# A perceiver layer pair on one core: top-query selection by index search, and experts chosen from un-normalised logits

## The chip, the cores and the metric

The kernel runs on one core of one Trainium2 chip. The metric is the device time of one launch in microseconds (us); 702.21 is the median of three runs (706.4, 702.21, 701.24).

A core has TensorE (PE: matmuls; PEld: its weight loads), VectorE (DVE), ScalarE (ACT), GpSimd (POOL) and SyncE (SP), each with a queue of its own that it works off in order, and 16 DMA engines. Matmul results go to eight PSUM banks of 128 x 512 float32.

## The reference, cut to what matters

Two batches of 256 rows, width 256, float32 throughout. Six residual sub-layers: cross-attention, a state-space layer, a spectral layer, a second cross-attention, a sparse self-attention, a mixture of experts. The change lies in the last two.

```python
# sparse self-attention, on xn = layernorm(x)
Q, K, V = proj(wq, bq), proj(wk, bk), proj(wv, bv)       # 16 heads of 16
scores = einsum('bhqd,bhkd->bhqk', Q, K) * scale
u = int(log(L))                                          # 5
top_u = top_k(scores.max(axis=-1), u)[1]
q_sel = take_along_axis(Q, top_u[..., None], axis=2)
attn = softmax(einsum('bhud,bhkd->bhuk', q_sel, K) * scale)
ctx = einsum('bhuk,bhkd->bhud', attn, V)
padded = zeros((B, H, L, d_k)).at[bi, hi, top_u].set(ctx)
x = x + (padded.transpose(0, 2, 1, 3).reshape(B, L, D) @ wo.T + bo)
...
# mixture of experts, on xn = layernorm(x)
logits = einsum('btd,ed->bte', xn, Wr)                   # 8 experts
probs = softmax(logits)
topk_vals, topk_idx = top_k(probs, 2)
router_weights = topk_vals / topk_vals.sum(-1, keepdims=True)
h = silu(einsum('btd,efd->btef', xn, W1))                # DFF 1024
y = einsum('btef,edf->bted', h, W2)
x = x + einsum('bte,bted->btd', gate, y)
```

## The kernel before

**Stages.** Layer 0's cross-attention over 4,096 keys fills the first 405 us, with batch 0's state-space layer woven in. Then come the other sub-layers up to the router, written as Python generators, one step up to each `yield`: stream `a` for batch 1 (state space, spectral, `context_layer`, `self_attention`, `router`), stream `b` for batch 0 (spectral onwards) and stream `m` (a matrix for the spectral layer). The string `ORDER` (L42) says whose step is issued next; a letter `w` issues a filler (`at_work`, L1543: a matmul whose result nobody reads). Instructions issued so keep this order on their engines (`in_order`). What comes behind, in the block of the experts, is placed by the framework's scheduler and may move ahead of it.

**Self-attention** (`self_attention`, L985). The rows are normalised (`normalised`), turned so that channels lie on partitions (`turned`: four transposes to PSUM and a copy), and projected (`ps_aqk`; query and key for half of the heads each time, weights packed in the tile `more`). Two masked copies of the queries make eight heads' scores from 32-partition matmuls (`ps_am`, 16 instructions of 256 columns); VectorE reduces each bank to its maxima (`reduce_max` into `m`, 16 a batch). `m` is turned (`ps_mt`) to 16 heads x 256 rows (`mt`). MAX8 finds the five highest, MATCH_REPLACE8 marks them, a scan numbers the marks, a matmul (`ps_st`) spreads them over 16 x 5 places, a compare gives `picked` (places x rows). `picked` is turned to `S`; a matmul gathers the rows of `xn` (`ps_xs`), another projects them (`ps_qs`). The scores stand with queries on partitions (`ps_sc`), so the maximum (`least`), exp and total run along the row, and the result is turned again (`ps_et`) before the values (`ps_ob`), the output weights (`ps_ow`) and the matmul that puts rows back (`ps_wo`). VectorE adds that to `x`.

**Router and dispatch** (`router`, L1527; L1579 on). The new rows are normalised into `xn5`, turned, projected to eight logits. With both batches done, the best two experts are found in two rounds over four row tiles (L1597 to L1604; `rank` breaks ties), matmuls with a triangle of ones count each row's place (`ps_n`), and for the first three experts (`DIRECT`) a compare and a matmul gather the rows of all four tiles (`direct`, `ps_xs`). Rows for the others go by eight indirect DMAs from POOL's queue to `x_slots` in DRAM and are fetched block by block.

**Experts.** Ten blocks of 128 rows: one for each of eight experts, and two of shared overflow parts. `hidden(k)` (L1749), then `output(k)` (L1789). Fourteen of the 32 weight halves (1 MB each, issued on SP's queue) are loaded ahead, into seven homes as these come free: `ctx0, ctx1, Q, K0, K2, K1, V1`, for experts 0 to 6 (L1505). `K1` held batch 0's attention weights in `context_layer`, `K2` is `more`. The other 18 halves go where a used one lay.

The planner's order for the streams is a fixed string; no due times are computed while the program is built.

Of the kernel before, what the change touches and what calls it, by code (L numbers as in the profile page):

```python
# [13 lines left out]
P = 128  # L14
# [4 lines left out]
NG = 4  # L19
# [24 lines left out]
        "mmabwbmmmabbaaaambamaamabmmmmmamabaamwmmmaaaaaaaabmmabababbbabaabwbbaaabwwaabbba",  # L44
        "abaabbbababaawaaaabbaaaaabbbaaaaaabaaaaaaaaaabbaaaaaaaaababaaaaaaabaaaaaaaaaaaaa",
        "aabaaaaaaabaaabaaaaaaaaaabbbaaaaaabaaaaabbababaabaaabaaaaaaabaaabbbbbabbbbabaaaa",
        "bbaaaababbbbaaaababababbaaababbabbbaaaabaaabababaaaaaaaabababababbaaabbaaabbbaba",
        "abbbbaabbbbaaaaaabaaabbbbbbaaaaaabbbaaaaaaaababaabbbaaaaababbbbaaaaaaaaawwwawaba",
        "waawwbaawbwbaaaaabaaaaaaawaabaaaaabaaaaaababaaabbaaabwwababaawabaabbbaabbaaabbaa",
        "bbabaabwbbwbbaaaawbbbaawwaaaaaaba",  # L50
# [16 lines left out]
def layers(ctx: ExitStack, tc: tile.TileContext, d: dict, out: bass.AP, general: bool):  # L67
# [244 lines left out]
    rank = route.tile([P, E], F32, tag="rank", name="rank")  # L312
# [6 lines left out]
    def route_constants(zeros):  # L319
        nc.gpsimd.memset(above, 1.0)  # L320
        nc.gpsimd.affine_select(
            out=above, in_=above, pattern=[[1, P]], compare_op=ALU.is_gt, fill=0.0, base=0, channel_multiplier=-1
        )
        nc.gpsimd.memset(ones, 1.0)
        for t, step, base in ((first_slot, P, 0), (rank, -1, E), (further, 1, 0), (beyond, ROOM, P)):
            nc.gpsimd.iota(
                t, pattern=[[step, t.shape[1]]], base=base, channel_multiplier=0, allow_small_or_imprecise_dtypes=True
            )
        nc.gpsimd.memset(zeros, 0.0)
        for k in range(NB):  # L330
            nc.gpsimd.dma_start(out=x_slots[k * P : (k + 1) * P, :], in_=zeros)
# [355 lines left out]
    nat = {}  # L687
# [130 lines left out]
    def context_layer(b, bank):  # L818
# [27 lines left out]
        room = STATE["more"][:, 1536:] if b else large("K1", "weights")  # L846
        pT = [room[:, 512 * i : 512 * (i + 1)].rearrange("p (c q) -> p c q", c=2) for i in range(4)]
# [74 lines left out]
    def picking(pool):  # L922


        expand = pool.tile([H, P], F32, tag="expand", name="expand")
# [30 lines left out]
        theirs = pool.tile([P, 2, P], F32, tag="theirs", name="theirs")  # L956
# [10 lines left out]
        which = pool.tile([1, P], F32, tag="which", name="which")  # L967
        biases = STATE["more"][:1, 1024 : 1024 + 2 * D]
        w = which.rearrange("p (g n) -> p g n", g=NG)
        nc.gpsimd.memset(which, -1.0)  # L970
# [6 lines left out]
        for u in range(TOP_Q):  # L977
            nc.gpsimd.memset(w[:, :, u : 4 * TOP_Q : TOP_Q], float(u + 1))
        turned_rows = pool.tile([P, 5], F32, tag="nth", name="nth")
        PICK.update(  # L980
            expand=expand, own=own, theirs=theirs, parity=parity, rowed=[which] + [biases[:, i * P : (i + 1) * P] for i in range(4)], turned=turned_rows,
            nth=turned_rows[:, :1], qb=turned_rows[:, 1:3], kb=turned_rows[:, 3:5],
        )

    def self_attention(b, bank):  # L985
# [17 lines left out]
        v, m = part(2, D), part(2, H)  # L1003
        mt, left, number = part(NQ + 8), part(NQ + 8), part(NQ)
        picked, S, XT = part(NQ), part(2, P), part(2, P)
        ve.tensor_tensor(of(b), of(b), rows[:, A1_BO, :].unsqueeze(1).to_broadcast([P, 2, D]), ALU.add)
        yield
        if b == 0:
            ps = bank("ps_nth")
            for i in range(5):  # L1010
                te.matmul(
                    ps[:, i : i + 1], lhsT=PICK["rowed"][i], rhs=ones[:1, :1], start=True, stop=True
                )
            yield
            ve.tensor_copy(PICK["turned"], ps[:, :5])
            yield
        for g in range(2):
# [24 lines left out]
            if g == 0:  # L1042
# [8 lines left out]
                yield  # L1051

        ve.memset(mt[:H, NQ:], LOWEST)
        ps = bank("ps_mt")
        for qt in range(2):
# [5 lines left out]
        ve.max(top, mt[:H])  # L1061
        ve.memset(top[:, TOP_Q:], LOWEST)
        ve.match_replace(left[:H], top, mt[:H], -LOWEST)
        ve.tensor_tensor(left[:H], left[:H], mt[:H], ALU.not_equal)
        yield
        ve.tensor_tensor_scan(
            number[:H], ones[:H, :1].to_broadcast([H, NQ]), left[:H, :NQ], 0.0, ALU.mult, ALU.add
        )
        ve.tensor_mul(number[:H], number[:H], left[:H, :NQ])
        yield  # L1070
        ps = bank("ps_st")
        te.matmul(ps[:, :NQ], lhsT=PICK["expand"], rhs=number[:H], start=True, stop=True)
        yield
        ve.tensor_scalar(picked, ps[:, :NQ], PICK["nth"], None, ALU.is_equal)
        yield
        ps = bank("ps_s")
        for t in range(2):
            te.transpose(ps[:, t * P : (t + 1) * P], picked[:, t * P : (t + 1) * P], ident)
        yield
        ve.tensor_copy(S.rearrange("p t n -> p (t n)"), ps[:, : 2 * P])  # L1080
        yield
        ps = bank("ps_xs")
        for c in range(2):
            for t in range(2):
                te.matmul(
                    ps[:, c * P : (c + 1) * P], lhsT=xn[:, t, c * P : (c + 1) * P], rhs=S[:, t, :],
                    start=(t == 0), stop=(t == 1),
                )
        yield
        ve.tensor_copy(XT.rearrange("p c n -> p (c n)"), ps[:, : 2 * P])  # L1090
        yield
        ps = bank("ps_qs")
        for g in range(2):
            for c in range(2):
                te.matmul(
                    ps[:, 64 * g : 64 * g + 64], lhsT=PICK["wq"][:, c, g * P : (g + 1) * P], rhs=XT[:, c, 64 * g : 64 * g + 64],
                    start=(c == 0), stop=(c == 1),
                )
        yield
        QS = S[:, 0, :]  # L1100
        ve.tensor_tensor(
            QS.rearrange("p (g n) -> p g n", g=2), ps[:, :P].rearrange("p (g n) -> p g n", g=2),
            PICK["qb"].unsqueeze(2).to_broadcast([P, 2, 64]), ALU.add,
        )
        QS = QS.rearrange("p (g s n) -> p g s n", g=2, s=2)
        ve.tensor_tensor(QS, QS, PICK["own"].unsqueeze(1).to_broadcast([P, 2, 2, 32]), ALU.mult)
        yield
        ps = bank("ps_sc")
        for g in range(NG):
            te.matmul(  # L1110
                ps[32 * g : 32 * g + 32, :NQ], lhsT=QS[:, g // 2, g % 2, :], rhs=KT[g // 2], start=True, stop=True
            )
        yield
        least = small.tile([P, 1], F32, tag="m1", name="least")
        ve.reduce_max(least, ps[:, :NQ], axis=AX.X)
        ve.tensor_scalar_mul(least, least, -1.0)
        yield
        e = XT.rearrange("p c n -> p (c n)")
        total = small.tile([P, 1], F32, tag="nb", name="total")
        se.activation(e, ps[:, :NQ], AF.Exp, bias=least, accum_out=total)  # L1120
        yield
        ve.reciprocal(total, total)
        ps = bank("ps_et")
        for t in range(2):
            te.transpose(ps[:, t * P : (t + 1) * P], e[:, t * P : (t + 1) * P], ident)
        yield
        ve.tensor_copy(S.rearrange("p t n -> p (t n)"), ps[:, : 2 * P])
        yield
        ps = bank("ps_ob")
        for c in range(2):  # L1130
            for t in range(2):
                te.matmul(
                    ps[:, c * P : (c + 1) * P], lhsT=v[:, t, c * P : (c + 1) * P], rhs=S[:, t, :],
                    start=(t == 0), stop=(t == 1),
                )
        yield
        ve.tensor_tensor(XT, ps[:, : 2 * P].rearrange("p (c n) -> p c n", c=2), PICK["theirs"], ALU.mult)
        yield
        ps = bank("ps_ow")
        for c in range(2):  # L1140
            te.matmul(ps[:, :D], lhsT=XT[:, c, :], rhs=a1_wo[:, c, :], start=(c == 0), stop=(c == 1))
        yield
        OW = QT[0][0]
        se.mul(OW, ps[:, :D], total)
        yield
        ps = bank("ps_wo")
        for t in range(2):
            te.matmul(ps[:, t * D : (t + 1) * D], lhsT=picked[:, t * P : (t + 1) * P], rhs=OW, start=True, stop=True)
        yield
        ve.tensor_tensor(of(b), of(b), ps.rearrange("p (t e) -> p t e", t=2), ALU.add)  # L1150
        yield
# [375 lines left out]
    def router(b, bank):  # L1527
        yield from normalised(of(b), xn5[:, 2 * b : 2 * b + 2, :])
        xnT = XNT(b)
        yield from turned(xn5[:, 2 * b : 2 * b + 2, :], xnT, bank("ps_tr"))  # L1530
        ps = bank("ps_r")
        for t in range(2):
            project_rows(ps[:, t * E : (t + 1) * E], xnT, t, wr)
        yield
        ve.tensor_copy(logits[:, 2 * b : 2 * b + 2, :], ps[:, : 2 * E].rearrange("p (t e) -> p t e", e=E))
        yield

# [5 lines left out]
    def at_work(n):  # L1543

        ps = bank("ps_work")
        for _ in range(n):
# [6 lines left out]
            spectral_layer(1, bank), later((context_rows, 1)), context(1, bank), self_attention(1, bank), router(1, bank),  # L1553
        ),
        "b": chain(
            spectral_layer(0, bank), later((context_rows, 0)), context(0, bank), self_attention(0, bank), router(0, bank),
# [22 lines left out]
    with pool("ffn", 1) as one:  # L1579
        gathered = large("P", "gathered")  # L1580
        room = big.tile([P, 4368], F32, tag="V0", name="room")

        warm = small.tile([P, 1], F32, tag="warm", name="warm")
# [442 lines left out]
```

## Time and profile before

| | us |
|---|---|
| median of three runs | 702.21 |
| the profiled execution | 701.64 |
| its span, first to last instruction | 699.9 |
| layer 0, up to | 405 |
| batch 1's second cross-attention ends, about | 540 |
| last of the score reductions ends | 564.4 |
| first expert matmul | 604.0 |
| first of eight row scatters | 602.0 |
| last block's output begins | 682.1 |

The page's slices are a fortieth of the span each. In a table of stages, PE busy time comes from matmuls whose ends are modelled, and `(x...)` counts instructions; a float32 matmul stands as two records. `PEclk` is the share of its clock that TensorE was granted. The chain of waits is followed back from the last instruction; "issue" in it is time in which an engine waited for nothing that the profile shows. Lines of most instructions here are those of one helper (L190), so groups are told apart by their tiles.

### The profile page before, as it was taken

To read this page: it belongs to the slowest core of one execution; us is meant where nothing else is said; L and a number is where in the kernel's file an instruction comes from. 1 tells how busy PE (TensorE), PEld (TensorE's weight loads), DVE (VectorE), ACT (ScalarE), POOL (GpSimd) and SP (SyncE) were. 2 spreads that over 40 slices of the span, in tenths; PEclk is the share of its full clock that TensorE was granted. 3 is DMA by queue.
4 is the path that set the end of the run, shared out by engine and by line. 5 is a ranking of instruction groups with operands and counts; after the bars stand their busy time and mean duration, and the time that the engine had idled before them with its cause. 6 is when DMAs were issued, how large, how long until landed. Compare 5 with 4: busy or idle time off the path is not lost.

```text
span 699.9 us, 15840 instructions
## 1 busy us (share of the span) xinstructions
PE 665.7 (95%) x6528; PEld 448.2 (64%) x6528; DVE 289.2 (41%) x716; ACT 365.6 (52%) x478; POOL 102.9 (15%) x170
## 2 busy tenths in 40 slices
PE   8999999999999999999999999999999888899994
PEld 6555555665455665555555577877877666899852
DVE  2221332121122465445445248765666865601112
ACT  3667655756767657767876847746333013111220
POOL 8400022300000000000002000124434000410012
PEclk9999999999999999999999999999999969999999
DMA  6520353310220001110010344000732406189982
GB/s 211 152 51 3 78 154 91 95 54 9 49 47 22 2 2 31 41 38 17 2 46 3 122 122 120 1 1 1 253 108 88 154 0 241 54 303 331 310 274 81
DMA packets 40178, 65.83 MB, mean 94 GB/s; under 512 B 6657, under 2 KB 26545, under 8 KB 39969
## 3 DMA queue, kind: packets, MB, share of 16 engines
q1 hardware_dynamic: 34608, 52.06, 23.8%
q0 software_dynamic: 3488, 10.83, 5.0%
q10 hardware_dynamic: 2000, 1.84, 0.8%
q8 instruction: 54, 0.88, 0.5%
q14 instruction: 28, 0.22, 0.1%
HBM read 52.12 MB, written 4.46 MB: 81 GB/s over the span
## 4 chain that ended last, share of the span: by engine, by line
PE 88%; DVE 6%; ACT 3%; issue 2%; DMA 1%; SPq 0%; DVEq 0%; ACTq 0%
PE av L190 21%; PE ps L190 21%; PE ps_y L1794 5%; PE ps_v L190 5%; PE ps_k L190 5%; PE ps_s L190 5%; PE ps_h L1754 4%; PE ps_in L190 2%; PE ps_ht L190 2%; DVE states L190 2%; DVE arest L190 1%; PE ps_work L190 1%; PE ps_q L190 1%; PE yps L190 1%; PE ps_h L1766 1%
## 5 line engine op out<-in xcount | busy, mean ns | idle before, releaser
L190 ACT ACTIVATE exps<-ps 128x1024 f32<-128x1024 f32 x256 | 248.0, 1021 | 121.1 <-PE ps L190 118.6
L190 PE MATMUL ps<-qk,KB 32*128 32x256 f32 x2048 | 156.8, 401 | 2.5 <-DVE mp L190 1.6
L190 PE MATMUL av<-exps,V 128*32 128x256 f32 x2048 | 137.6, 385 | 0.3 <-ACT exps L190 0.3
L190 PEld LDWEIGHTS ps<-qk,KB 32*128 32x128 f32 x2048 | 99.8, 184 | 51.9 <-issue 41.0
L190 PEld LDWEIGHTS av<-exps,V 128*32 128x32 f32 x2048 | 53.5, 109 | 66.5 <-issue 39.9
L190 DVE TENSOR_TENSOR_SCAN states<-decay,ps_in 128x256 f32<-128x256 f32 x64 | 40.2, 671 | 21.0 <-PE ps_in L190 21.0
L190 DVE COPY V<-ps_v 128x512 f32<-128x512 f32 x28 | 19.4, 692 | 63.5 <-PE ps_v L190 61.6
L190 DVE COPY qk<-ps_k 128x512 f32<-128x512 f32 x28 | 19.3, 689 | 63.3 <-PE ps_k L190 42.3
L1794 PE MATMUL ps_y<-w,room 128*128 128x256 f32 (+1 forms) x256 | 39.2, 380 | 2.8 <-issue 2.5
L190 PEld LDWEIGHTS ps_v<-l_wv,ctxT 128*128 128x128 f32 x256 | 30.9, 191 | 10.4 <-issue 8.1
L190 PE MATMUL ps_v<-l_wv,ctxT 128*128 128x128 f32 x256 | 36.4, 287 | 0.4 <-ACT head L190 0.4
L1794 PEld LDWEIGHTS ps_y<-w,room 128*128 128x128 f32 (+1 forms) x256 | 28.6, 151 | 11.2 <-issue 6.2
L190 PE MATMUL ps_k<-ctxT,wkc 128*128 128x512 f32 x64 | 35.3, 638 | 0.0
L1754 PE MATMUL ps_h<-room,w 128*128 128x128 f32 x256 | 32.1, 283 | 2.7 <-issue 2.6
L1774 ACT ACTIVATE room<-ps_h 128x512 f32<-128x512 f32 x16 | 9.4, 597 | 47.3 <-PE ps_h L1754 30.5
L190 PE MATMUL ps_s<-xn,ctxT 128*128 128x256 f32 x128 | 33.4, 383 | 0.0
L190 POOL TENSOR_TENSOR weights<-weights 128x512 f32<-128x512 f32 x15 | 19.0, 1268 | 97.0 <-ACT weights L190 96.8
L1754 PEld LDWEIGHTS ps_h<-room,w 128*128 128x128 f32 x256 | 30.9, 198 | 3.6 <-issue 3.4
L190 ACT ACT_TABLE_LOAD x16 | 20.5, 1283 | 15.6 <-DVE least L190 14.8
L190 PEld LDWEIGHTS ps_s<-xn,ctxT 128*128 128x128 f32 x128 | 23.5, 190 | 5.8 <-issue 3.0
L190 POOL TENSOR_TENSOR more<-more 128x512 f32<-128x512 f32 x15 | 19.0, 1267 | 24.2 <-ACT more L190 24.1
L190 ACT ACTIVATE more<-more 128x512 f32<-128x512 f32 x16 | 10.1, 630 | 23.4 <-DVE more L190 23.4
(387 smaller groups left out, 814.1 us busy)
## 6 DMA issues: line engine op xcount, KB each, us to landing
w<-in_moe_w SPq DMA_DIRECT2D x32, 1024.0 KB
KB<-qk SPq DMA_DIRECT2D x224, 32.0 KB
ctxT<-in_ctxT POOLq DMA_DIRECT2D x4, 512.0 KB
ctxT<-in_ctxT SPq DMA_DIRECT2D x1, 2048.0 KB
x_slots<-O POOLq DMA_DIRECT2D x14, 128.0 KB
ctxT<-in_ctxT SPq DMA_DIRECT2D x3, 512.0 KB
y_slots<-room ACTq DMA_DIRECT2D x8, 128.0 KB
rows<-in_rows POOLq DMA_DIRECT2D x1, 896.0 KB
```

Of the source, the lines that this page charges most:

```text
L190: i = getattr(self.engine, name)(*args, **kw)
L1754: nc.tensor.matmul(ps[fc // 4][:, (fc % 4) * P : (fc % 4 + 1) * P], lhsT=weights[k, 0, 0][0][:, c, fc * P : (fc + 1) * P], rhs=xT[k][:, c, :],
L1766: nc.tensor.matmul(ps[i][r, :], lhsT=xT[k][:, c, r], rhs=weights[k, j, 0][0][:, c, 512 * i : 512 * (i + 1)], start=(c == 0), stop=(c == 1),)
L1774: nc.scalar.activation(to[i], ps[i], AF.Silu)
L1794: nc.tensor.matmul(ps[r, :D], lhsT=hT[k][:, fc, r], rhs=weights[k, j, 1][0][:, fc, :], start=(fc == 0), stop=(fc == NF - 1),)
```

## The change

The queries are no longer found again from gathered rows. After the maxima, an index search gives each head's five row numbers; these are spread over the 80 places by a product and a matmul with ones, and compared with the rows' own numbers (`place`): that is `S` at once. Queries are projected for all rows beforehand (`q`) and selected by `S`. The scores are made with keys on partitions, so that exp's output goes into the value matmul without a turn; the (negated) maximum, known from the search, is added by a matmul, and the totals come from a matmul with ones. The residual is added in PSUM (`new`), by a matmul with the identity.

The logits come ahead of the norm: `wr` less its column means makes the mean drop out, and the row's scale doesn't change which experts are highest. They are the sum of the old rows' logits (`old`, the turned rows before attention) and the picked places' own (`owr`, the output weights times the router's). The scale (`inverse`) enters in the softmax. Each batch chooses, counts and gathers inside its own stream; batch 0's gather for the three direct experts lies in `K1`'s old room until batch 1's is added. `ORDER` is a new string: 306 letters `a` for 311, 157 `b` for 158, 20 `m` as before, 5 `w` for 24; the two runs of four fillers around `ps_n` are gone, too. Nothing in layer 0 or in the experts' blocks is edited.

```diff
@@ picking
-        expand = pool.tile([H, P], F32, tag="expand", name="expand")
+        masks = acts.tile([P, 2, D], F32, tag="O0", name="masks").rearrange("p c n -> p (c n)")
+        expand = masks[:H, :P]
...
+    def self_weights(bank):
+        ps = bank("ps_nth")
+        for i in range(4):
+            te.matmul(ps[:, i : i + 1], lhsT=PICK["rowed"][i], rhs=ones[:1, :1], start=True, stop=True)
+        for c in range(2):
+            te.matmul(ps[:, E : 2 * E], lhsT=ones, rhs=wr[:, c, :], start=(c == 0), stop=(c == 1))
...
+        yield from turned(a1_wo, woT, bank("ps_woT"))
+        ps = bank("ps_owr")
...
@@ self_attention, after the value projection of the first half
+                ps = bank("ps_aq")
+                for t in range(2):
+                    project_rows(ps[:, t * D : (t + 1) * D], xnT, t, PICK["wq"])
+                yield
+                se.copy(q, ps.rearrange("p (t e) -> p t e", t=2))
+                yield
+                yield from turned(of(b), old, bank("ps_old"))
@@ self_attention, after mt
-        ve.max(top, mt[:H])
-        ve.memset(top[:, TOP_Q:], LOWEST)
-        ve.match_replace(left[:H], top, mt[:H], -LOWEST)
...
+        ve.max(top, mt[:H, :NQ])
+        ve.max_index(at, top, mt[:H, :NQ])
+        ve.tensor_scalar_mul(top, top, -1.0)
...
+        te.matmul(ps[:, :P], lhsT=ones[:H, :], rhs=spread[0], start=True, stop=True)
+        yield
+        for t in range(2):
+            ve.tensor_scalar(S[:, t, :], ps[:, :P], PICK["place"][:, t : t + 1], None, ALU.is_equal)
...
+        for t in range(2):
+            for g in range(2):
+                te.matmul(
+                    sc[:, t * P + 64 * g : t * P + 64 * g + 64], lhsT=KT[g][:, t * P : (t + 1) * P],
+                    rhs=QS[:, 64 * g : 64 * g + 64], start=False, stop=(t == 1 and g == 1),
+                )
+        pk = bank("ps_pk")
+        for t in range(2):
+            te.transpose(pk[:, t * P : (t + 1) * P], S[:, t, :], ident)
+        yield
+        e = QT[1][1]
+        se.activation(e, sc[:, : 2 * P], AF.Exp)
+        ve.tensor_copy(picked, pk[:, : 2 * P])
...
-        se.activation(e, ps[:, :NQ], AF.Exp, bias=least, accum_out=total)
...
+        ps, new = bank("ps_lg0"), bank("ps_new")
+        for t in range(2):
+            project_rows(ps[:, t * E : (t + 1) * E], old, t, PICK["wr"])
...
+        te.matmul(new.rearrange("p (t e) -> p t e", t=2), lhsT=ident, rhs=of(b), start=True, stop=False)
...
+        pr, po = bank("ps_or"), bank("ps_ow")
...
+        se.activation(root, total, AF.Sqrt)
...
-    def router(b, bank):
...
+    def attention_and_router(b, bank):
+        lg, new = yield from self_attention(b, bank)
...
+        for t in range(2):
+            ve.max(two[:, t, :], logits[:, 2 * b + t, :])
+        ve.tensor_copy(best[:, ts, :TOP_E], two[:, :, :TOP_E])
+        for t in range(2 * b, 2 * b + 2):
+            ve.match_replace(rest[:, t, :], best[:, t, :], logits[:, t, :], -LOWEST)
+        ve.tensor_tensor(chosen[:, b, :2, :], rest[:, ts, :], logits[:, ts, :], ALU.not_equal)
+        yield
+        nr = bank("ps_n")
...
+        for t in range(2):
+            ve.tensor_scalar(
+                xn5[:, 2 * b + t, :], new[:, t * D : (t + 1) * D], mv[:, t, 0:1], r[:, t : t + 1], ALU.subtract, ALU.mult
+            )
+        se.copy(of(b), new.rearrange("p (t e) -> p t e", t=2))
...
+        for k in range(1, DIRECT):
+            spots(b, k)
+            yield
+            ps = gather(b, k, bank)
+            yield
+            gathered_to(b, k, ps)
...
+    def gathered_to(b, k, ps):
+        first = XS["room"][:, k * D : (k + 1) * D]
+        if b:
+            ve.tensor_tensor(place_of_x(k), first, ps[:, :D], ALU.add)
+        else:
+            se.copy(first, ps[:, :D])
@@ the experts' block
-        for i in range(TOP_E):
-            of_these = rest if i else lg
-            nc.vector.reduce_max(best[:, i, :], of_these, axis=AX.X)
...
-        at_work(4)
-        ps = bank("ps_n")
...
-        direct(0)
...
+        num = XS["counts"]
```

## The prediction

> **What bounds the kernel now.** First the page: engines, the clock row and the chain.
>
> ```profile
> PE 665.7 (95%) x6528; PEld 448.2 (64%) x6528; DVE 289.2 (41%) x716; ACT 365.6 (52%) x478; POOL 102.9 (15%) x170
> ...
> PEclk9999999999999999999999999999999969999999
> ...
> PE 88%; DVE 6%; ACT 3%; issue 2%; DMA 1%; SPq 0%; DVEq 0%; ACTq 0%
> ```
>
> TensorE carries the whole program, and one slice of forty has a lower clock. The diff leaves everything up to 405 us alone (layer 0) and everything after the first hidden matmul. So next, busy time by stage for what lies between (columns: window, its length, then PE, PEld, DVE, ACT, POOL, clock, DMA share, GB/s):
>
> ```profile
> sum 135.00, PE 130.44 PEld 106.03 DVE 87.50 ACT 68.41 POOL 38.03; mean PE 21.74 PEld 17.67 DVE 14.58 ACT 11.40 POOL 6.34
> 560.00:564.00 4.00, 1.51 (x10) 1.08 (x10) 4.00 (x8) 0.00 (x0) 0.00 (x0) 1.00 0.00 0
> 564.00:568.00 4.00, 3.50 (x14) 2.83 (x14) 3.54 (x12) 0.00 (x0) 0.00 (x0) 0.62 0.00 0
> 568.00:578.00 10.00, 9.62 (x41) 7.12 (x40) 3.43 (x12) 1.85 (x3) 0.00 (x0) 0.50 0.05 3
> 615.00:640.00 25.00, 25.00 (x167) 23.50 (x167) 2.55 (x6) 4.18 (x7) 2.50 (x5) 0.98 0.98 339
> 640.00:680.00 40.00, 40.00 (x326) 30.96 (x324) 4.51 (x10) 8.02 (x14) 1.91 (x3) 1.00 0.93 310
> ```
>
> The sum is of 405 to 540: TensorE is dense there. From 540 it is not: VectorE is full in 560 to 564, and then TensorE runs at half clock for some 14 us. Last, the chain of waits from 540 (start, length, what):
>
> ```profile
> 539.75 0.98 PE ps_total L190 x8
> ...
> 541.70 3.04 PE ps_work L190 x14
> ...
> 559.16 5.20 DVE arest L190 x9
> ...
> 595.38 1.28 PE ps_n L190 x10
> ...
> 598.49 5.36 PE ps_xs L190 x48
> ...
> 603.96 4.91 PE ps_h L1754 x43
> 608.87 0.37 issue
> ```
>
> Three marks follow from it: C = 539.75, where batch 1's cross-attention is summed; R = 564.36, where the last score reduction ends (559.16 + 5.20); T = 603.96, the first hidden matmul. The prediction is where C, R and T fall.
>
> **C: from 405 to the end of cross-attention.** I laid both order strings against the generators' yields, letter by letter. When batch 1's last `weigh` is called, batch 0 has been given 15 of its 16 score reductions before, and 8 after. TensorE loses, ahead of C: `ps_nth` 1.20, the second `ps_aqk` 1.74, two `ps_am` at 1.08, `ps_av` 1.92, and three filler letters (14 records took 3.04, so 0.43 for two): 8.3 us. It gains `self_weights`: 12 records of one to eight columns at 0.12 (`ps_nth`'s own 1.20 for ten), the turned output weights 0.72 (`ps_tr`), eight records for their product 0.97 (`ps_r`): 3.1. As TensorE is 97% dense, C moves by 5.2, to 534.5. The other bounds: the new order may fill worse or better than the 4.6 us idle in 135; I take plus or minus 3. POOL's mask building loses five small fills and gains one fill and one iota; its 2.6 busy us in 425 to 450 wait for nothing: nothing, and under 1 us if uncovered.
>
> **R: from C to the last reduction.** Before, C to the first masked query (549.17) took 9.5. After it is the same steps; batch 0's query, key and old-row projections (1.73 + 0.57 + 1.74) fit in TensorE's wait for the norm, which fillers held; I add 0.5. So masked queries start at 544.5. From there VectorE has in order: 22 reductions at 0.62 (17 were 10.5 us busy), 13.6; four masked queries, 2.0; batch 1's value sum 0.68; batch 0's `mt` copy 0.41, search 1.47 (below), two places 0.56, masked selected queries 0.45: 19.2. Before, the like stretch (549.2 to 564.4) held 14.5 of VectorE work in 15.2; with two hand-overs to TensorE more I add 2 and get R = 565.8. So R stays: what C wins goes into reductions that came out from under cross-attention.
>
> The search is MAX8 (0.42 in its row), an index find that the trace doesn't show, a negation 0.15 and two products of 16 rows, 0.22 each. MATCH_REPLACE8 on the same row took 0.40 with a value load of 0.08; the find is bounded by 0.2 (a tiny instruction) and 1.2 (three passes of 0.40); I take 0.45, for it too is one pass.
>
> **T: from R to the first hidden matmul.** Before this is 39.6. Batch 1's chain after, each by its nearest row: turn 0.38, copy 0.41, search 1.47, places' matmul 0.3, compare 0.56, queries by selection 0.97, mask 0.45, scores 0.9, exp 0.47, values 1.05, mask 0.41, output and router rows 1.3, scaling 0.47, logits 0.44, choice of experts 1.3 (seven instructions at 0.17 to 0.20), norm statistics 1.6 beside the rank matmuls 0.8, number and root 0.2, compare 0.56, normalise 0.74, gather 0.97, copy 0.42: 15.4. Two more compares, gathers and copies overlap to 4.5. About 30 hand-overs at 0.05 are 1.5; one table load, for exp after the other batch's root, 1.28 (bounds 0 and three, 3.8). Batch 0's tail, which the order sets ahead of it, takes 1.7 at the start and 1.8 in between. Sum 26.2: T = 592.0.
>
> What went: second transposes, the gather of rows before projecting, the row maximum, the logits' detour over the normalised rows (transpose, copy, projection: about 2.2), the two-round choice (592.6 to 595.3), one third of the dispatch, and the half clock, worth some 6. ScalarE gains three copies at 0.58 and a root at 0.20 a batch; it is busy 13 of 76 us behind 540, so nothing, and 2 if each stood in a chain. TensorE's extra work, 6 us a batch (query projection 1.73, old rows turned 0.57, residual into the sum 0.86, old logits 0.97, router rows and logits 0.9, totals 0.44, and smaller ones), lies beside VectorE's reductions or in the other batch's waits; uncovered it would cost 6. Bank waits aren't shown before; nothing to 2.3 (TensorE's wait for `ps_xs`), taken as nothing, since eight banks remain.
>
> **Behind T.** I keep 95.9, with the stall at 608.87 to 613.5 while the eight row scatters are issued, and its second clock dip; it may change by 4 either way. Moved behind T: expert 5's two weight halves. Their home is now the room for spots and gathers until the last copy; before, they were issued at 499 and 501. So 20 halves of 1.05 MB instead of 18; at the 310 to 339 GB/s above, 62 to 68 us, while the last is needed at the final output, 682.1, or 78 after T. Covered; if that cover went, they'd cost 6. On SP's queue they meet the eight reads of expert numbers (601.6 to 607.8 before, 0.6 to 1.2 each); behind both wait only the later halves, first needed 51 after T (expert 7). The scatters on POOL's queue still hang on batch 1's counts: some 15 small instructions at 0.2 after the ranks, shared with the compares on VectorE, set their start near 590, two ahead of T as before (602.0), so the first fetch behind them keeps its place. Batch 1's `more` room comes free earlier, so expert 4's halves leave 576.5 for about 555, where the DMA share is 0.
>
> Span: 699.9 - 11.9 = 688. The profiled execution took 701.64, 1.74 over its span, and the median is 0.57 above that: **690 us**.
>
> [...] The row: with 1.51 us of matmuls in 4 us and a longest gap of 2.26, the clock fell. [...] My longest gaps behind R are under 2 us with over half of each 4 us busy, so by the row too I take no closing.
>
> In 604 to 616 the scatters had the DMA engines to themselves, at a share of 0.31. [...]
>
> **Rivals.**
> - *The clock closes and stays closed (slower).* Place: 553 to T and on into the first hidden block. Two such dips stand in the profile. Price: TensorE has about 28 us of work there, so 28 more: 718. It decides once more than some 19 us of that work is at half clock; a single closing of 14 us costs 7 (697). Against: fewer long waits, work spread over the stretch. 0.08, and 0.12 for the single one.
> - *The tail doesn't overlap.* With batch 0 later, the two chains take turns on VectorE and the banks, and the extra 6 us shows: 696 to 699. For: VectorE alone has some 45 us between C and T. 0.12.
> - *Order better than that:* the first hidden block slips in ahead of the last two gathers, -4, and the stall shrinks, -4: 682; 0.10.
> - *The change only shuffles* (search as long as the old numbering, logits as late): T back at 600 to 604, 698 to 702: 0.05.
>
> **How the numbers follow.** My forecast, 684 to 695, has 0.53; the better order 0.10; the rest above. Faster by over 1% (below 695.2; 1% is about what a measurement of this kernel tells from no change): 0.53 + 0.10 + half of the single dip and half of the missing overlap, 0.12 = 0.75. Within 1%: their other halves and the shuffle, 0.17. Slower by over 1%: 0.08. The range 678 to 704 leaves out the lasting closure and the far ends of the better order and of the shuffle, some 0.12.
>
> **What would show it.** Batch 1's context sum near 534; last reduction near 566; first hidden matmul at 588 to 594; full clock from 550 to T; no wait on a weight in the last stage. It is wrong if the clock row shows halves there, if the index find takes over 1 us, or if the stretch before 534 has grown.

## The result, and the profile after

The changed kernel takes 713.39 us, the median of four runs (713.83, 713.4, 710.88, 713.38), against 702.74 for four runs of the kernel before: a ratio of 1.0136, interval 1.009 to 1.0182. It is slower by about 1.4%, where 690 us, a gain, was forecast. The profiled execution took 713.83, its span 711.8. In the ratios of e2 and e3 below, runs over 1.5% above the fastest of the same kernel (four of ten and two of ten) are left out; the spread of all ten is told there.

First the page: TensorE's row, the clock row, and the shares of the chain.

```profile
PE 673.9 (95%) x6520; PEld 457.5 (64%) x6520; DVE 284.9 (40%) x726; ACT 370.9 (52%) x486; POOL 102.6 (14%) x165
...
PEclk9999999999999999999999999999999955979997
...
PE 84%; DVE 5%; DMA 4%; issue 2%; ACT 2%; POOL 1%; SPq 0%; ACTq 0%; DVEq 0%; POOLq 0%
```

VectorE lost 4.3 us of work, as the change intends. But two slices of the clock row stand at 5 and two at 7, where before one stood at 6, and DMA has 4% of the chain where it had 1%. Busy time by stage shows both (window, length, then PE, PEld, DVE, ACT, POOL, clock, DMA share, GB/s):

```profile
405.00:540.00 135.00, 127.99 (x758) 103.78 (x751) 80.45 (x188) 69.89 (x127) 38.32 (x30) 1.00 0.22 69
...
560.00:564.00 4.00, 4.00 (x23) 3.39 (x22) 2.65 (x5) 1.27 (x3) 0.00 (x0) 1.00 0.00 0
564.00:568.00 4.00, 2.72 (x26) 1.84 (x24) 3.46 (x11) 1.66 (x2) 0.00 (x0) 0.95 0.72 239
568.00:578.00 10.00, 10.00 (x50) 8.10 (x49) 5.49 (x12) 0.38 (x1) 0.00 (x0) 0.50 0.34 114
578.00:602.00 24.00, 24.00 (x85) 19.14 (x84) 8.54 (x39) 5.11 (x7) 0.00 (x0) 0.50 0.26 88
615.00:640.00 25.00, 16.28 (x100) 14.82 (x100) 5.60 (x17) 2.99 (x5) 8.93 (x11) 0.80 0.84 316
```

From 568 to 602 the clock is at a half without a break, 34.1 us for the 13.7 of before; TensorE counts as fully busy there, and VectorE is busy for 14.0 of the 34. From 615 to 640 TensorE was dense before and now stands still for 8.7 us. Last the chain (start, length, what):

```profile
541.07 0.79 PE ps_total L190 x8
...
565.01 1.24 PE ps_am L190 x16
...
588.75 3.05 PE ps_sc L190 x10
...
606.51 5.25 PE ps_xs L190 x40
...
613.55 1.05 POOL x_slots L1755
...
622.57 6.18 DMA x_slots<-xn,at
628.88 0.51 issue
629.39 5.34 DMA room<-x_slots
```

`ps_sc`, ten records, takes 3.05 us there; at full clock (e1 below) it takes 1.66. Behind the first hidden matmul the chain runs over the eight scatters on POOL's queue, the landing of the last (6.18 us) and the first fetch (5.34), for which the turn of the fourth expert's rows waits.

The prediction's marks, with the first exp of layer 0 as a fifth, since it came 2.3 us later in this execution although nothing of the change precedes it. e1 is the first experiment:

| us | before | predicted | after | e1 |
|---|---|---|---|---|
| first exp of layer 0 | 20.5 | 20.5 | 22.8 | 22.3 |
| C, batch 1's cross-attention summed | 539.7 | 534.5 | 540.9 | 541.6 |
| R, last score reduction | 564.4 | 565.8 | 576.8 | 576.6 |
| T, first hidden matmul | 604.0 | 592.0 | 611.7 | 599.8 |
| end of the span | 699.9 | 688 | 711.8 | 702.0 |

### The profile page after: what moved, and what is told of

Same layout as the page of the kernel before. It is cut to its first block, busy times and chain, and to the rows that moved or that the text cites. A ratio compares the mean times of both kernels' runs of the same rounds, so it can differ in the third digit from the quotient of the medians.

```text
span 711.8 us, 15847 instructions
## 1 busy us (share of the span) xinstructions
PE 673.9 (95%) x6520; PEld 457.5 (64%) x6520; DVE 284.9 (40%) x726; ACT 370.9 (52%) x486; POOL 102.6 (14%) x165
## 3 DMA queue, kind: packets, MB, share of 16 engines
q1 hardware_dynamic: 34608, 52.06, 23.2%
## 4 chain that ended last, share of the span: by engine, by line
PE 84%; DVE 5%; DMA 4%; issue 2%; ACT 2%; POOL 1%; SPq 0%; ACTq 0%; DVEq 0%; POOLq 0%
PE av L190 21%; PE ps L190 20%; PE ps_k L190 5%; PE ps_v L190 5%; PE ps_s L190 5%; PE ps_y L1874 4%; PE ps_h L1834 3%; DVE states L190 2%; PE ps_ht L190 2%; PE ps_in L190 2%; PE ps_am L190 2%; PE ps_q L190 1%; PE ps_aqk L190 1%; POOL x_slots L1755 1%; PE ps_new L190 1%
## 5 line engine op out<-in xcount | busy, mean ns | idle before, releaser
L1834 PE MATMUL ps_h<-xT,w 128*128 128x128 f32 x256 | 29.8, 275 | 0.0
L1834 PEld LDWEIGHTS ps_h<-xT,w 128*128 128x128 f32 x256 | 29.5, 192 | 0.2
L190 DVE TENSOR_REDUCE arest<-ps_am 128x2 f32<-128x512 f32 x32 | 20.1, 683 | 5.7 <-PE ps_am L190 5.7
L190 PE MATMUL ps_ht<-ident,states 128*128 128x128 f32 x128 | 20.4, 281 | 1.6 <-DVE states L190 1.6
```

Source lines behind the costliest of these rows:

```text
L190: i = getattr(self.engine, name)(*args, **kw)
L1834: nc.tensor.matmul(ps[fc // 4][:, (fc % 4) * P : (fc % 4 + 1) * P], lhsT=weights[k, 0, 0][0][:, c, fc * P : (fc + 1) * P], rhs=xT[k][:, c, :],
```

## The experiments

**e1: nine fillers back, ahead of the dip.** The theory: the clock closes at 564 to 568, where little stands on TensorE, and stays closed because the fillers are gone. The edit is to `ORDER` alone; a filler's result is read by nobody.

```diff
-...waabaabbbabaaabaaaaabbbaaabab...
+...wwabaawwbwwbbabwwaaabaaaaawwbbbaaabab...
```

> Nine filler matmuls added to the changed kernel, all ahead of the place where its clock fell (around 568) or just behind it; nothing else. Theory 'gate' (the loss behind the end of cross-attention is the half clock, 568 to 602, begun by one sparse stretch): the clock row stays full there, the first hidden matmul comes 10 to 16 us earlier than 611.7, time 698 to 704. Theory 'chain' (VectorE and hand-overs set the pace, the half clock is only seen beside them): first hidden matmul within 3 us of 611.7, time 711 to 714. Theory 'mix' (the new matmuls with few columns close the gate wherever it is): clock full to about 585, then half, time 706 to 711.

702.5 us over ten runs, ratio to before 1.0000 (0.998 to 1.0019), where the changed kernel has 1.0136: about 10 us less. Two stretches of e1 (columns as above):

```profile
564.00:568.00 4.00, 3.72 (x28) 2.46 (x26) 2.25 (x8) 1.76 (x2) 0.00 (x0) 1.00 0.54 160
...
568.00:602.00 34.00, 32.26 (x233) 28.00 (x234) 25.72 (x123) 11.22 (x21) 0.35 (x1) 1.00 0.31 106
```

The clock is full from 413 to 618; the same 34 us hold 233 matmul records where after the change they held 133. R didn't move (576.6), and R to T fell from 34.9 to 23.2. With the nine fillers back the loss against before is gone; that they act by the clock, and not by some other way, is what e9 below shows.

**e2: the room for spots and gathers in another buffer**, so that expert 5's two weight halves load early.

```diff
-        if not b:
-            XS["room"] = room
+        if "room" not in XS:
+            XS["room"] = large("P", "xroom")
```

> The changed kernel with batch 0's gather room in the home P, so that K1 is free early and expert 5's halves are issued near 500 as before. Theory 'contention' (TensorE's wait of 8.7 us for the fetched rows behind the second block comes from expert 5's 2 MB running beside the scatters): the wait falls under 2 us, last stage 100 -> 92 to 96, time 705 to 709. Rival (the scatters start 2 us behind the first hidden matmul instead of 2 ahead, and that alone makes the rows late): the wait stays over 5 us, time 711 to 714.

Ratio 0.9997 (0.997 to 1.0024), but that is of six runs. All ten have a median of 705.12 and spread from 698.67 us at a granted clock of 0.987 to 713.08 at 0.959; the profiled one (712.57) has the long dip, 569.6 to 600.4. There TensorE still stood 7.2 us at 625: expert 5's load is not the main cause of that wait. That one program's runs have such different granted clocks is taken up under e9.

**e3: the order of before for the first 299 letters, the new one behind them**, that is, until batch 0's cross-attention is added to `x`. In this diff and the next the strings are written short: `OLD` and `NEW` are the two orders, `steps_left` what the new one has beyond those letters.

```diff
-ORDER = NEW
+ORDER = OLD[:299] + steps_left(NEW, OLD[:299])
```

> The changed kernel with the old order string up to the end of batch 0's cross-attention and the new one behind it. Theory 'front' (the new string's start fills TensorE worse, 3 us more idle in 405 to 450): batch 1's context sum 3 to 5 us earlier, time 708 to 711. Rival (what the front wins is lost again in the stretch to the last reduction): the context sum earlier, time 712 to 714.

699.43 us, ratio 0.9946 (0.9914 to 0.9979), nine of ten runs from 694.23 to 704.92 and one at 712.21. Neither expectation held: C did not come earlier (542.1). What was won is the clock, at a half for one short piece only (570.6 to 574.0) between C and T, 598.95. Behind C the fillers are those of the changed kernel, none more, so this owes much to chance: by the count below, the half-clocked window at 570.6 sums to 1,554, a hair over the line, where the like one of e2 (569.6) sums to 1,472 and the clock stays at a half for 30.7 us.

**e4: the kernel before without any filler.**

```diff
-        at_work(4)
-ORDER = OLD
+ORDER = OLD.replace("w", "")
```

> The kernel before without any of its 24 filler letters and the two runs of four; nothing else. Theory 'gate': half clock for over 25 us instead of 14, time 707 to 716. Theory 'chain': the fillers only fill, half clock about as before, time 700 to 703.

711.96 us, ratio 1.0132 (1.0115 to 1.0149). The old kernel, too, owes about 10 us to its fillers: without them it has half clock at 546.0 to 552.8, 566.4 to 583.5 and 593.8 to 607.4. It also shows the wait for the fetch, 6.9 us at 625.6, with none of the change in it.

**e5 and e6: fillers, and weight halves later.** The first halves for freed rooms to be loaded behind the third hidden block; e6 has the room of e2 too.

```diff
+            if (k, i) in ((0, 0), (1, 0), (0, 1)):
+                put_off.append((k, i))
+                return
+            load_next(k, i)
+            while put_off:
+                load_next(*put_off.pop(0))
```

> The nine fillers of e1, and the weight halves for the freed rooms of the first two blocks issued only behind the third hidden block, the room of which is first, so that SP's queue waits there. Contention theory: in e1 the last scatter's landing took some 7 us from its issue because weight halves ran beside it (before the change, with none running, 3); without them the first fetched block is issued 3 to 4 us earlier, TensorE's gap of 9.1 us near 614 shrinks to about 5, and the time falls by 3 to 5 us against e1's 702.5, to 698 or 699. Rival (issue-bound): the eight scatters' issue on POOL's queue, 8 x 1.27 us, sets the fetch alone; the gap stays at 9 and the time within 1 us of e1. Second rival: the halves issued later arrive too late further on, a wait on a weight appears before the last blocks and the time is above e1's.

> As e5, and the room for spots and gathers lies in another buffer, so that expert 5's two halves are loaded early and not beside the scatters. Contention theory: no weight moves in the first 11 us behind the first hidden block, the scatters land as before the change (3 us), the gap is 4 to 5 us and the time 1 to 2 us below e5. Rival: expert 5's halves have landed before the last scatters anyway, same as e5 within 1 us.

e5: 703.14 us, 1.0015 (0.9994 to 1.0036). It told nothing of its theory: behind the streams the framework's scheduler places instructions, and it issued a half at the end of each of the first blocks as before (601.96, 605.54, 608.99). e6: 700.14, 0.9963 (0.9946 to 0.9981), with a gap of 6.7 us for e1's 9.1, so expert 5's halves cost some 2 us, and not in the scatters: the fetch follows the last one by 7.5 (7.2 in e1), but lands in 2.7 us where e1's took 5.3. e10 does what e5 was meant to do.

**e7: e1 with batch 1's query projection and turned old rows behind its last scores.**

```diff
-                ps = bank("ps_aq")
...
-                yield from turned(of(b), old, bank("ps_old"))
+                if b == 0:
+                    ps = bank("ps_aq")
...
+            elif b:
+                ps = bank("ps_aq")
...
+                yield from turned(of(b), old, bank("ps_old"))
```

Four letters `a` of `ORDER` move with them.

> e1 with batch 1's projection of all queries and its turned old rows (four steps, some 2.3 us of TensorE) moved behind its last scores. Theory (TensorE has become the bound between the cross-attention's end and the last score reduction): the last reduction ends 2 us or more earlier than e1's 576.6, and the first hidden matmul 1 to 2 us earlier than 599.8; time 700.5 to 701.5. Rival (hand-overs between VectorE and the masked queries set that stretch, TensorE's extra work lies beside): the last reduction stays within 0.7 us of 576.6 and the time within 1 us or above e1, since the moved steps then stand in batch 1's chain.

717.55 us, ratio 1.0207 (1.019 to 1.0224). Taking 2.2 us off TensorE shortened C to R by 1.1 (35.0 to 33.9): TensorE is only in part the bound there. The rest of the loss came from the clock, and neither theory had it. The chain of e7:

```profile
574.49 1.74 PE ps_aq L190 x8
576.23 0.02 issue
576.25 1.07 ACT arest L190 x2
577.34 1.28 ACT L190
578.63 0.39 ACT arest L190
```

The moved copies and a table load (1.28) on ScalarE stand ahead of batch 0's exp; TensorE waits 2.4 us, and the clock is at a half from 580.9 to 604.8.

**e8: e3's front, e1's fillers, e2's room, e5's edit.**

> The order of e3 up to the cross-attention's end, with e1's nine fillers, e2's room and the late weight halves of e5. If the gains add: e3's 699.4, less 3 to 5 for the fetch wait, and none of its longer runs since the clock is held: 694 to 697, ratio 0.988 to 0.993. If e3 gained from the short dips' absence alone and the fetch wait is issue-bound: 699 to 700.

700.17 us, 0.9959 (0.9933 to 0.9984). The gains do not add: with e5's edit undone by the scheduler the gap stayed at 7.8 us.

**What the clock counts.** In all these profiles every inner piece at half clock lasts a whole number of 3.413 us: before, 13.653 (4) and 3.413 (1); after, 34.133 (10) and 10.240 (3); e7, 23.893 (7). Within a profile the changes, too, lie whole steps apart (before: 564.96, 578.61, 612.74, 616.15 and 698.08). So I cut each span into windows on that grid. For each window I summed its matmul records, each as columns x (rows / 128) x (weight columns / 128), a record across an edge split by time. In the ten profiles taken so far, from layer 0's end (408 us) to some 10 us before the span's end, 1,553 or more is followed by full clock and less by a half in 816 of 817 windows, 73 of them followed by a half. The 1,553 was read off these same windows: the highest sum with a half behind it is 1,542, the lowest with full clock, but for the one exception (1,489), 1,553. Three runs (window start, clock in it, the sum); e9 is the next experiment:

```
after                     e1                        e9
560.8  1.0  3745          563.4  1.0  3364          560.2  1.0  3804
564.2  1.0  1282  closes  566.8  1.0  2651          563.6  1.0  2972
567.6  0.5   701          570.2  1.0  2428          567.1  1.0  1124  closes
571.1  0.5  1542          573.6  1.0  2573          570.5  0.5   652
574.5  0.5  1014          577.0  1.0  2133          573.9  0.5  1504
577.9  0.5  1104          580.4  1.0  1701          577.3  0.5  1202
...                       ...                       ...
594.9  0.5   562          594.1  1.0  2774          584.1  0.5  1341  opens
598.4  0.5  1591  opens   597.5  1.0  3400          587.5  1.0  1755
```

The highest sum of any window at full clock is some 4,100, at half clock some 2,100. So the clock reopened here behind half-clocked windows that were about three quarters full of full-height work (1,553 of 2,100), while at full clock about three eighths held it (1,553 of 4,100). The stretch of the two short chains, with matmuls of 8 to 64 columns or of 32 rows, stays below that though it counts as fully busy: after the change nine windows in a row, from 567.6 on, sum to 562 to 1,542 each, and the clock, lowered behind the sparse window at 564.2 (1,282), stays down. At 571.1 the changed kernel missed by 11 columns in 1,553, by this count.

**e9: the nine fillers made thin.** The test of that count against recorded busy time. The nine fillers of e1 call this helper instead of `at_work`.

```diff
+    def at_work_thin():
+        ps = bank("ps_work")
+        te.matmul(ps[:, :D], lhsT=ident[:32, :], rhs=rows[:32, LN_G, :], start=True, stop=True)
```

> e1 with its nine fillers made thin: 32 of the 128 rows, the same 256 columns, the same number, places and recorded time. From the ten profiles so far: cut into the clock row's own grid of 3.413 us, a window is followed by full clock where its matmul records, each as columns x rows/128 x weight columns/128, come to 1,553 or more, by half clock below, in 816 of 817 windows. Work theory: a thin filler counts a quarter (128 of 512), so the clock closes near 565 and stays closed as without fillers: half clock 24 to 34 us before the first hidden matmul, time 711 to 714. Rival (recorded busy time counts): the clock stays open as in e1, 701 to 704.

711.18 us, ratio 1.0081 (1.0049 to 1.0113) where e1 has 1.0000. Three stretches of e9, the last one the window that closed the clock:

```profile
564.00:568.00 4.00, 3.91 (x30) 2.89 (x30) 2.26 (x8) 1.76 (x2) 0.00 (x0) 1.00 0.51 141
568.00:585.00 17.00, 17.00 (x74) 12.79 (x74) 7.06 (x16) 0.38 (x1) 0.00 (x0) 0.57 0.26 91
...
567.06:570.47 3.41, 3.41 (x24) 2.79 (x20) 2.20 (x8) 0.00 (x0) 0.00 (x0) 1.00 1.02 396
```

TensorE is recorded busier in 564 to 568 than in e1 (3.91 for 3.72), and busy without a break in the window that closes the clock; it closes all the same, for 17.07 us (5 windows), where I had expected 24 to 34. In the four profiles taken after the 1,553 was set down, it errs in the same stretch for one window of 322: e9's 584.1 opens the clock with 1,341. Busy time as the measure is refuted; that rows count is shown, the exact weighting is not.

Over the whole spans the count errs for 13 of 2,829 windows of the fourteen profiles, always with full clock behind too low a sum. Eleven of them are filled mostly by matmuls with 32 weight columns: at 404 to 407, the end of layer 0, 1,235 and more held the clock while 1,201 and less lowered it, and before's last output held it with 567 (684.4). So for such matmuls the count is off, in a way that no run here settles.

Why the runs of e2 differ so in their clock isn't shown. The grid stands elsewhere in each of the three profiled executions listed above (windows start at 564.2, 563.4 and 563.6), but where it stood in each run of e2, their times alone don't show.

**e10: e6 with the loads held in written order on SP's queue.**

```diff
+        if k >= LOADED:
+            tc.keep_in_program_order(load)
```

> As e6, with the weight loads behind the first hidden block now kept in the written order on SP's queue; in e5 and e6 the program's order had not held and the loads were issued at each hidden block's end as in e1. First load some 11 us behind the first hidden matmul, none beside the first seven scatters. Contention theory: the fetch follows the last scatter's issue by 3 us (e6: 7.5), TensorE's gap of 6.7 us shrinks to 2 or 3, time 695 to 698. Rival (the last scatter's landing takes 7 us whatever else moves): gap 6 to 7, time 699 to 701, or above, where later weights are waited for.

700.65 us, 0.9963 (0.9928 to 0.9998): no faster than e6, and not the 695 to 698 expected. First e6's last scatter, its first fetch and the matmul that waits for it, from the list of instructions; then the chain of e10, at the scatters and in the tail:

```profile
610.92 0.97 POOL L1755 DMA_INDIRECT x_slots<-xn,at  x1 [0.30 <-issue]
...
618.46 1.68 POOL L1816 DMA_DIRECT2D room<-x_slots  x3 [6.57 <-DMA x_slots<-xn,at]
...
621.25 0.66 PE L1821 MATMUL ps_xs<-ident,room 128*128 128x128 f32 x2 [6.73 <-DMA room<-x_slots]
```

```profile
609.06 0.97 POOL x_slots L1757
...
612.12 5.82 DMA room<-x_slots
...
679.85 0.80 issue
...
683.23 1.04 issue
```

The fetch follows the last scatter's issue by 3.05 us where e6 had 7.5, TensorE's gap is 3.8 for 6.7, and the dip behind it is gone. So weight loads beside the scatters delay their landing: that part of the theory holds. But the loads held back (611.59 and on) now run beside the fetch, whose rows arrive 5.8 us behind its issue where e6 took 2.7. The rest of the gain goes in two short stalls in the hidden blocks (0.38 and 0.83 us, 609.7 to 611.5) and in the tail: the gathers start 3.3 us sooner after T, while TensorE still works on the last blocks; it stands still for five short waits put down to issue, 2.7 us together, and the clock is at a half from 684.4 to 691.2.

**e11: the row numbers' chain and the scatters written ahead of batch 1's gathers**, with e1's fillers and e2's room; **e12** adds four fillers behind batch 1's first gather.

```diff
         se.copy(of(b), new.rearrange("p (t e) -> p t e", t=2))
+        if b and not general:
+            dispatch()
         yield
```

> e6's fillers and room, loads as in e1; the row numbers' chain (14 small VectorE instructions) and the eight scatters are written into batch 1's stream ahead of its three gathers. Place theory: scatters start some 4 us earlier, near 597.5 to 598, two ahead of the first hidden matmul, which comes 1 to 3 us later (601 to 603); the fetch wait of 7 to 9 us goes to 0 to 3 and the clock's dip behind it to nothing: 693 to 697. Rival (the stall seen before the change, 608.9 to 613.5, comes back whenever scatters start ahead of the first hidden matmul): TensorE stands still some 4 us inside the first hidden block, 698 to 701.

> e11 with four full-row fillers behind batch 1's first gather, where TensorE stood still 2.5 us and the clock halved for two windows (595.8 to 602.6) ahead of the first hidden matmul. Work theory: four fillers are 2,048 of the 1,553 that a window needs, the clock stays, the first hidden matmul comes some 2.5 us earlier than e11's, and no fetch is waited for: 697 to 698.5, below e6's 700.1 and e11's 700.6. Rival: the fillers and the wait that follows only shift the place: within 1 us of e11.

e11: 700.57 us, 0.9954 (0.9919 to 0.9989), not the 693 to 697 expected. The wait for the fetch is gone and T to the end is 94.7 us, the shortest of all; but T came at 603.46, 5 us later against C than in e1, since TensorE waits 2.5 us for VectorE at 592 and the clock halves for two windows (that at 592.4 sums to 1,024). e12: 701.39, 0.9966 (0.9942 to 0.999), not the 697 to 698.5 expected. The fillers held the clock there, but C to T shrank by only 1.3, and the stall inside the first hidden block came back in small pieces (0.73, 0.38 and 0.47 us at 607 to 610; that window sums to 1,440, and the clock closes once more).

No version beats the kernel before by more than about half a per cent: e3 to e12 apart from e4, e5, e7 and e9 lie between 0.9946 and 0.9966, and their intervals overlap.

## Why the prediction was wrong

**The step that failed: "by the row too I take no closing".** The place was named (553 to T) and the mechanism was the first rival, at 0.08; its price of 718 was for 28 us of work at half clock, and 34 us of half clock cost about 10 (e1). What misled was the measure: longest gaps under 2 us and over half of each 4 us recorded busy. I asked it of the stretch behind R alone, while the clock fell 9 us ahead of R; but it would have passed there, too. The window that closed the clock after the change (564.2) had TensorE recorded busy for 2.14 of 3.41 us, with a longest gap of 0.71; in e9 the closing window was busy throughout. The count over the grid could have been made from the profile of before alone: its dip starts behind a window that sums to 1,111 and ends behind one of 1,568. The windows that closed the clock in these dips were not idle, only below about three eighths of full-height work: 1,111 (before), 1,282 (after) and 1,124 (e9) of some 4,100. The full clock that the sum of 26.2 takes is shown by no run of the change without more fillers: from C to T it is at a half for 34.1 us after the change, 30.7 in e2 and 3.4 in e3.

**C: 5.2 us forecast, 0.8 won** (540.9, less the 2 us that layer 0 came later, against 539.7), outside my plus or minus 3. TensorE's busy time between layer 0's last exp and C fell by 3.2 (130.0 to 126.8) instead of 5.2, and its idle time grew from 4.3 to 6.8. The bound on how the new order fills was too narrow; e3, with the old order up to the sum of batch 0's cross-attention and its fillers, has 4.8 idle but 130.2 busy, and no earlier C either.

**R: 31.3 us from C forecast, 35.9 measured**, and 35.0 in e1 at full clock, so the clock explains only 0.9 of it. In e1 the masked queries start 6.4 behind C, sooner than the 10.0 forecast. VectorE's work from there is 21.5 us for 19.2: 24 reductions for 22, at the 0.62 a piece that I took (14.9 for 13.6), and six masked queries for four (3.15 for 2.0). The term that failed is the 2 us for hand-overs: VectorE stands idle for 7.1 us between the first masked query and R (8.1 after), while TensorE is idle for only 2.1 between C and R. One place is in the chain of e1, batch 0's projections and then batch 1's first, one behind the other on TensorE, with two hand-overs between (start, length, what):

```profile
543.57 1.73 PE ps_aq L190 x8
545.29 0.44 PE ps_old L190 x4
545.73 1.74 PE ps_aqk L190 x8
547.50 0.48 ACT arest L190
548.00 0.55 DVE arest L190
548.60 1.15 PE ps_am L190 x16
549.75 1.94 PE ps_aqk L190 x8
```

"TensorE's extra work lies beside VectorE's reductions" was thus half wrong: e7 says that 2.2 us of it are worth 1.1.

**R to T: 26.2 forecast, 23.2 in e1, 34.9 after.** At full clock the sum of the chain by nearest rows holds and errs on the safe side. The index search is right: the find took 0.41 and a value load 0.08, for 0.45 forecast between 0.2 and 1.2; negation 0.16, products 0.22.

**Behind T: 95.9 kept, 100.1 measured**, just outside my plus or minus 4. Its stall of 4.6 us at 609 did go, but the scatters start 1.8 behind T instead of 2 ahead of it, since the chain of row numbers shares VectorE with the gathers' compares and the shares. "The first fetch behind them keeps its place" failed with that, and the loads' meeting with the scatters, which I left at nothing for want of a row, is 4.5 us of landing (7.5 in e6, 3.05 in e10). The row that I read for it, 604 to 616 of the old profile, has the scatters alone only until 613.6, when a weight half was issued. Why loads beside the scatters delay them, no run shows.

The other rivals: "the change only shuffles" holds for e1's time, by chance of equal sums; "the tail doesn't overlap" is refuted by 23.2. "Slower by over 1%" had 0.08, and 713.39 lies 9 us above the range's upper end.

What stays open: why the old kernel's stall inside the first hidden block comes and goes with the scatters' start, how matmuls with 32 weight columns count for the clock, and how much of C to R is order and how much is new work.

## What to carry to other kernels

Before taking filler matmuls out, cut the profile into the clock's own windows and sum each one's matmul work by rows and columns, not by busy time: a window near the line is a risk (the profiles of e2 and e3 differ by 82 columns in one window, and by 27 us of half clock behind it), and a stretch of short chains that follows it may not reopen the clock by itself (after the change, nine windows of 562 to 1,542 didn't). What is saved on VectorE beside a dense TensorE need not show: here 4.3 us of VectorE's work are gone, and no version is more than about half a per cent faster. When a step is moved behind a mark, ask which DMAs will be under way beside it: here the fetch behind a scatter went from 3 us to about 7.

## Not expected of the hardware

- In these profiles the clock changed on a grid of 3.413 us and, behind layer 0, was full behind windows of 1,553 full-height columns or more and at a half behind less (816 of 817 windows of ten profiles). One program has runs of 699 and of 713 us, at granted clocks of 0.987 and 0.959 (e2).
- Nine matmul pairs of 256 columns, some 5 us of work, are worth about 10 us (ratios 1.0136 and 1.0000); the same nine on 32 rows less than half of that (1.0081).
- Layer 0's first exp comes at 20.5 to 21.0 us in five of the profiled executions (before, e5, e8, e10, e11) and at 22.1 to 22.8 in the other nine, though layer 0 is the same in all; the difference still stands at its last exp (404.3 to 404.6, and 405.7 to 406.3).
- While eight row scatters or gathers are issued, 1.27 us apart, TensorE's queue can stand still in pieces of 0.3 to 1.05 us that no semaphore explains (before, e9, e10, e11, e12), and in other runs doesn't (after, e1, e6).
